# A selective scan on one core: dt's positive part and logarithm added up by TensorE, input scaling split in two places, SyncE's loads in written order

## The chip, the cores and the metric

The kernel runs on one core of a Trainium2 chip. The metric is device time in microseconds (us), from three runs of the unchanged kernel; lower is better. A core has TensorE (PE, matrix products into PSUM), VectorE (DVE), ScalarE (ACT), GpSimd (POOL) and SyncE (SP, which here only issues DMAs).

## The reference, cut to what matters

Four layers work on an image of shape (3, 256, 48, 48); the first three are an attention block and two 3x3 convolutions. The change touches only the fourth, a Mamba-style scan over the 2304 pixels of each image, with 512 inner channels and 16 states per channel:

```python
u  = silu(conv4(x_in))
dt = softplus(dt_raw @ dt_proj_w.T + dt_proj_b)
dA = exp(dt[:, :, None] * A)
h  = h * dA + dt[:, :, None] * B[:, None, :] * u[:, :, None]     # one step per pixel
y  = einsum('bdn,bn->bd', h, C) + u * D
out = (y * silu(z)) @ out_proj_w.T
```

The softplus is computed as log(1 + exp(x)) = max(x, 0) + log(1 + exp(-|x|)).

## The kernel before, in words

**Chunks and places.** The scan layer is cut into 18 chunks of 384 pixels (3 images x 6). A chunk runs 8 steps, one for each pair (m, h) of a block m of 128 channels and a half h of the states. A step does 8 scans on VectorE (`scan`, L1817), each of 385 columns. The text counts 16 places j in a chunk, four scans each: `j = 4*m + 2*h + part//4`. "Scan 13.0" is the first scan of place 13.

**The loop around a scan.** ScalarE makes the decay factors that a scan reads (`decay`, L1809: exp of dt times A) into one of three PSUM slots. A slot is free again when the scan that reads it has ended, so a decay can be at most three scans ahead. GpSimd and VectorE fill the scan tiles with dt*u*B before the scans (`fill`: L1779 and L1783 on GpSimd, L1765 on VectorE), and GpSimd multiplies the scanned states by C (`times_c`, L1834). TensorE adds the states up (L1851), and VectorE gates the sum (L1858).

**The next chunk's preparation** is spread over the scans of the current one. The list `plan` names for every stage its place j, its position in the place and how many chunks ahead it works. The positions are BEGIN, MID, DONE and LATE, after the place's scans 0, 1, 2 and 3, and PE_, after LATE (in odd places: at the step's end, after the filling and `times_c`). The stages that matter here, for the chunk one ahead:

- `project_dt(k, m0)` multiplies into the two PSUM banks `ps_g` for the channel blocks m0 and m0+1 (m0 is 0 or 2).
- `softplus(k, m0)` is on ScalarE: Abs of the two banks into `k.dt` (L1327), Exp (L1328) and Ln (L1329) of both at once.
- `take_dt(k, m0)` is on VectorE, for each of the two banks: max(x, 0) + logarithm back into the bank (L1343), then the bank times `k.u` into `k.dtu` (L1344), and three filler matmuls (`keep_busy`, L1336).
- `keep_dt(k, m0)` copies the banks to `k.dt` on ScalarE (L1349) and stores `k.dt` and three quarters of `k.dtu` in DRAM through SyncE's queue (`dtd`, L1353; `dtud`, L1355).
- `spread` (L1714) reads `dtd` and `dtud` back with rows repeated, eight DMAs on SyncE's queue for each m; `spread_second` (L1722) reads four more.

For the chunk two ahead, `group_scale` (L1213) applies a scale and shift to the input tile `xg`, one ScalarE operation for each of the two channel halves; `less_mean` (L1222) and `centre` (L1235, L1237) subtract the mean, using the same two banks `ps_g`.

**Fillers.** `keep_busy` issues 128x128 matmuls on the identity whose result nobody reads; the dictionary `busy` gives their places in the scan loop.

**Order.** `keep_order` binds each instruction of the scan layer on TensorE, VectorE, ScalarE and GpSimd to the one written before it, so these engines run in written order. SyncE is not in its list before the change. Waits between engines and on DMAs are set by the tile framework from what each instruction reads and writes; an instruction that overwrites a tile waits until a DMA that was issued earlier in the program has finished reading it. The first chunk is prepared before the layer starts (`early_preparation`, with the old `softplus` and `take_dt`), so the stages of `plan` that work one chunk ahead run 17 times.

Of the kernel before, what the change touches and what calls it, by code (L numbers as in the profile page):

```python
# [11 lines left out]
AF = mybir.ActivationFunctionType  # L12
ALU = mybir.AluOpType
# [3 lines left out]
P = 128  # L17
# [3 lines left out]
CT = 2  # L21
# [63 lines left out]
def net(  # L85
# [21 lines left out]
    nc = tc.nc  # L107
# [18 lines left out]
    ident = const.tile([P, P], F32, name="ident")  # L126
# [105 lines left out]
    listed = nc.cur_bb.bb.instructions  # L232
# [148 lines left out]
    with ExitStack() as l0:  # L381
# [36 lines left out]
        with ExitStack() as p1:  # L418
# [15 lines left out]
            for b in ORDER:  # L434
# [23 lines left out]
                for c in range(NCH):  # L458
                    for m, dst in ((0, y1), (1, cur[b])):
                        pm = ps.tile([P, 512], F32, tag="s", name="ps_y")  # L460
                        for ct in range(CT):
                            nc.tensor.matmul(  # L462
                                pm[:, :CH], ws[:, ct, m * P : (m + 1) * P], chunk(xb[:, ct, :], c),
                                start=ct == 0, stop=ct == CT - 1,
                            )
                        if c == 0 and m == 0:
# [3 lines left out]
                            bias=bb[:, m : m + 1], scale=b1sc[:, m : m + 1],  # L470
# [64 lines left out]
        with ExitStack() as p2:  # L535
# [9 lines left out]
            for i in range(NB):  # L545
# [400 lines left out]
                for mt in range(0, NT, 2):  # L946
                    pv = pair()
                    for j in range(2):
                        nc.tensor.matmul(
                            pv[:, j, :384], cur[2][:, (mt + j) * P : (mt + j + 1) * P], wn[2],  # L950
                            start=True, stop=True,
# [5 lines left out]
                mark = listed[-1]  # L957
# [3 lines left out]
                if exact:  # L961
                    k1 = keys(1)
                    attend_exact(2, k2)
                    k0 = keys(0)
                    attend_exact(1, k1)
                    attend_exact(0, k0)
                    at_once(mlp_weights(i, 2))
                    at_once(mlp_weights(i, 1))
                else:
                    attention({2: k2})  # L970
                    keep_order(tc, listed, mark)
# [76 lines left out]
        mark = listed[-1]  # L1048
# [45 lines left out]
        for _ in mixing:  # L1094
            pass
        keep_order(tc, listed, mark)
        for steps in small_steps:
            at_once(steps)
# [11 lines left out]
    def room(k, name):  # L1110
        return rooms[name][k.at % len(rooms[name])]
# [94 lines left out]
    bank = [t[:, :CH] for t in whole]  # L1206

    def group_scale(k):  # L1210
        sc, sh = norm3[k.b]
        for ct in range(CT):
            nc.scalar.activation(  # L1213
                k.xg[:, ct, :], k.xg[:, ct, :], AF.Identity,
                bias=sh[:, ct : ct + 1], scale=sc[:, ct : ct + 1],
            )
# [80 lines left out]
    def take_dbc(k):  # L1297

        dbc = k.dbc = room(k, "dbc")
        nc.scalar.activation(  # L1300
            dbc, bank[0][:96], AF.Identity, bias=ident[:96, DTR : DTR + 1]
        )
        bcd = dram.tile([2, DS, CH], F32, name="bcd")
        k.bc = []
        for j in range(2):
            nc.sync.dma_start(bcd[j], dbc[32 * (j + 1) : 32 * (j + 1) + DS, :])
            t = room(k, f"bc{j}")
            for i in range(4):
                src = bcd[j].rearrange("(g i) n -> i g n", i=4)[i : i + 1]
                nc.sync.dma_start(t[32 * i : 32 * i + 32], src.broadcast_to([32, 4, CH]))  # L1310
            k.bc.append(t)
        k.dt = room(k, "dt")
        k.dtu = room(k, "dtu")

    def project_dt(k, m0):
        for j in range(2):
            m = m0 + j
            nc.tensor.matmul(
                bank[j], w3v["dtsb"][:, m * P : (m + 1) * P], k.dbc[: DTR + 1, :],
                start=True, stop=True,  # L1320
            )

    def softplus(k, m0):

        both = k.dt[:, m0 : m0 + 2, :]
        for j in range(2):
            nc.scalar.activation(k.dt[:, m0 + j, :], bank[j], AF.Abs)  # L1327
        nc.scalar.activation(both, both, AF.Exp, scale=-1.0)  # L1328
        nc.scalar.activation(both, both, AF.Ln, bias=1.0)  # L1329
# [3 lines left out]
    def keep_busy(src, times):  # L1333

        for i in range(times if spread_tiles else 0):
            nc.tensor.matmul(  # L1336
                spread_tiles[-1][:, i % 2, CH:], ident, src, start=True, stop=True
            )

    def take_dt(k, m0):  # L1340
        for j in range(2):
            m, pdt = m0 + j, bank[j]
            nc.vector.scalar_tensor_tensor(pdt, pdt, 0.0, k.dt[:, m, :], ALU.max, ALU.add)  # L1343
            nc.vector.tensor_tensor(k.dtu[:, m, :], pdt, k.u[:, m, :], ALU.mult)  # L1344
            keep_busy(k.dtu[:, m, :P], 3)

    def keep_dt(k, m0):
        for j in range(2):
            nc.scalar.copy(k.dt[:, m0 + j, :], bank[j])  # L1349
        if m0 == 0:  # L1350
            k.dtd, k.dtud = {}, {}
        d = k.dtd[m0] = dram.tile([P, 2, CH], F32, name=f"dtd{m0}")
        nc.sync.dma_start(d, k.dt[:, m0 : m0 + 2, :])  # L1353
        d = k.dtud[m0] = dram.tile([3 * P // 4, 2, CH], F32, name=f"dtud{m0}")
        nc.sync.dma_start(d, k.dtu[P // 4 :, m0 : m0 + 2, :])  # L1355
# [27 lines left out]
    def store(k, mo):  # L1383
        nc.scalar.copy(k.ot[:, mo, :], k.y_out[mo])
        nc.sync.dma_start(
            out[k.b, mo * P : (mo + 1) * P, k.c * CH : (k.c + 1) * CH], k.ot[:, mo, :]
        )
# [2 lines left out]

    BEGIN, MID, DONE, LATE, PE_ = range(5)
    plan = [
        (12, MID, 2, group_scale),
        (12, PE_, 2, less_mean),
        (13, DONE, 2, centre),
        (13, PE_, 2, lambda k: keep_busy(ident, 5)),
        (13, PE_, 2, square_mean),
# [19 lines left out]
        (7, LATE, 1, lambda k: silu(k.u)),  # L1417
        (8, BEGIN, 1, project_u),
        (8, LATE, 1, take_dbc),
        (8, PE_, 1, lambda k: project_dt(k, 0)),  # L1420
        (9, LATE, 1, lambda k: softplus(k, 0)),
        (10, DONE, 1, lambda k: take_dt(k, 0)),
        (10, LATE, 1, lambda k: keep_dt(k, 0)),
        (10, PE_, 1, lambda k: project_dt(k, 2)),
        (11, LATE, 1, lambda k: softplus(k, 2)),
        (12, MID, 1, lambda k: take_dt(k, 2)),
        (12, DONE, 1, lambda k: keep_dt(k, 2)),
    ]

    after = [  # L1430
# [27 lines left out]
    def early_preparation():  # L1458
# [7 lines left out]
        while 2 not in norm3:  # L1466
            yield
        group_scale(k)
        yield
        less_mean(k)  # L1470
# [33 lines left out]
        for stage in (group_scale, less_mean, centre, square_mean, inverse_root, normalise):  # L1504
            stage(k)
            yield
# [7 lines left out]
        project_u(k)  # L1514
        yield
        take_dbc(k)
        yield
        for m in (0, 2):
            project_dt(k, m)
            yield  # L1520
            softplus(k, m)
            yield
            take_dt(k, m)
            yield
            keep_dt(k, m)
            yield
# [162 lines left out]
    with ExitStack() as l3:  # L1689
# [35 lines left out]
        def spread_pe(k, m):  # L1725

            t = psr.tile([P, 2, 512], F32, name="ps_r")
            for q in range(2):
# [10 lines left out]
        steps = [(at, m, h) for at in range(len(todo)) for m in range(DI) for h in range(2)]  # L1739
        tiles = {}  # L1740
        state = {}
        busy = {(2, 0, 3): 4, (2, 1, 1): 3, (2, 1, 2): 3, (2, 1, 3): 3, (2, 1, 5): 3,
                (3, 0, 0): 3, (3, 0, 1): 3, (3, 0, 2): 2}

        parts_of_step = [(g, q) for a in range(2) for g in range(2) for q in (2 * a, 2 * a + 1)]
        slots = [psd.tile([P, 512], F32, name=f"ps_da{i}") for i in range(3)]
# [113 lines left out]
        mark = listed[-1]  # L1860
        last = len(todo) - 1
        k = chunks[0]
# [7 lines left out]
        for s, (at, m, h) in enumerate(steps):  # L1870
            if m == 0 and h == 1 and at + 2 <= last:
                fetch(at + 2)
            for part in range(8):
                j = 4 * m + 2 * h + part // 4
# [38 lines left out]
        k = chunks[last]  # L1913
# [5 lines left out]
        for mo in range(2):  # L1919
            project_y(k, mo, DI - 1, DI)  # L1920
            store(k, mo)
        keep_order(tc, listed, mark)
    late_pools.close()


def keep_order(tc, listed, mark):

    engines = (
        mybir.EngineType.PE, mybir.EngineType.DVE, mybir.EngineType.Activation,
        mybir.EngineType.Pool,  # L1930
    )
    before = {}
    start = next(i for i in reversed(range(len(listed))) if listed[i] is mark)
    for ins in reversed(listed[: start + 1]):
        if ins.engine == mybir.EngineType.Activation:
            before[ins.engine] = ins.name
            break
    for ins in listed[start + 1 :]:
        e = ins.engine
        if e not in engines:  # L1940
            continue
        if e in before:
            tc.add_manual_dep(
                ins, before[e],
                mybir.DependencyInfo(mybir.DependencyClass.NoSync, mybir.DependencyReason.DATA),
                reason="order",
            )
        before[e] = ins.name


def net_kernel(tc, *args):

    with tc.tile_pool(name="flag", bufs=1) as pool:
        flag = pool.tile([1, 1], I32, name="flag")
        net(tc, *args, flag, False)
        bad = tc.nc.values_load(flag[:1, :1])
        with tc.If(bad > 0):
            net(tc, *args, None, True)
# [77 lines left out]
```

## Time and profile before

| what | value |
|---|---|
| median of 3 runs | 3374.56 us (3373.80 to 3378.72) |
| the profiled execution's own time | 3369.03 us |
| its span, first to last instruction | 3367.3 us |
| scans of the last layer, first to last start | 2013.8 to 3343.6 us |
| busy in 2300 to 2500 us: VectorE, GpSimd, PE, ScalarE | 198.5, 190.9, 186.4, 168.1 us |
| granted TensorE clock, whole span | 0.982 |

The scan layer takes about 1330 us, 74 us for each of the 18 chunks. Busy times of engines overlap and don't add up. A busy PE is not a PE at its peak, since matmuls are pipelined.

### The profile page before, as it was taken

How to read it: one execution, taken by the hardware profiler on the slowest of the kernel's cores; microseconds unless marked ns; L12 is line 12 of the kernel's file. 1: busy time of each engine (PE TensorE's matmuls, PEld its weight loads, DVE VectorE, ACT ScalarE, POOL GpSimd, SP SyncE). 2: the span in 40 equal slices, each digit the busy share in tenths (PEclk: the TensorE clock that was granted, in tenths of full speed). 3: DMA queues.
4: the chain of work that ended last, by engine and by line, in shares of the span. 5: the costliest groups of instructions: out<-in, count | busy, mean ns of one | idle time of the engine just before them, and what ended most of it. 6: DMA issues, size and time to landing. Idle time of an engine off the chain costs nothing.

```text
span 3367.3 us, 54979 instructions
## 1 busy us (share of the span) xinstructions
PE 3151.7 (94%) x21314; PEld 1586.5 (47%) x21314; DVE 2899.6 (86%) x3302; ACT 2375.1 (71%) x3596; POOL 1335.3 (40%) x457
## 2 busy tenths in 40 slices
PE   7999999999999999979999988999999999999985
PEld 4334343452333434547777764444444444444442
DVE  4799989959988997379976459999999999999997
ACT  3688888838888886332233548888888888888874
POOL 0000000000000000220000009999999999999997
PEclk9999999999999999989999999999999999999998
DMA  4000000010000002566611044555545555555552
GB/s 174 23 8 10 8 8 6 8 46 4 8 7 8 10 8 71 193 210 214 218 38 38 19 120 107 125 127 129 143 123 141 133 129 123 130 130 134 135 131 56
DMA packets 182165, 290.84 MB, mean 86 GB/s; under 512 B 34738, under 2 KB 148466, under 8 KB 179971
## 3 DMA queue, kind: packets, MB, share of 16 engines
q1 hardware_dynamic: 168658, 267.15, 29.6%
q10 hardware_dynamic: 13232, 20.06, 1.8%
q8 instruction: 169, 2.77, 0.4%
q14 instruction: 106, 0.86, 0.1%
HBM read 236.24 MB, written 50.64 MB: 85 GB/s over the span
## 4 chain that ended last, share of the span: by engine, by line
PE 52%; DVE 32%; ACT 7%; DMA 4%; issue 4%; SPq 1%; POOL 0%; ACTq 0%; DVEq 0%; POOLq 0%
DVE hs L1817 21%; PE ps_s L638 16%; PE acc L651 14%; PE ps_c L1546 8%; DVE hs L1765 3%; DVE u L296 2%; PE ps_y L462 2%; PE ps_m L665 2%; ACT ps_da L1809 2%; PE ps_s L1031 2%; PE ps_m L711 1%; PE acc L529 1%; PE ps_s L518 1%; DVE ps_g L1343 1%; DMA dtr<-dtd 1%
## 5 line engine op out<-in xcount | busy, mean ns | idle before, releaser
L642 ACT ACTIVATE pt<-ps_s 128x1024 f32<-128x1024 f32 x972 | 942.4, 1022 | 154.8 <-PE ps_s L638 142.1
L1817 DVE TENSOR_TENSOR_SCAN hs<-ps_da,hs 128x385 f32<-128x385 f32 x1152 | 1002.6, 936 | 5.1 <-ACT ps_da L1809 2.4
L857 DVE TENSOR_TENSOR part<-part,pt 128x2048 f32<-128x2048 f32 x396 | 906.6, 2289 | 41.2 <-ACT pt L642 18.5
L1809 ACT ACTIVATE ps_da<-dtr,u 128x384 f32<-128x384 f32 x1152 | 656.3, 582 | 191.3 <-DVE hs L1817 182.7
L164 POOL TENSOR_TENSOR rstd<-ve,mhalf 128x2 f32<-128x2 f32 (+1 forms) x26 | 16.3, 629 | 1473.4 <-DVE ve L162 1473.4
L638 PE MATMUL ps_s<-q,kt 32*128 32x512 f32 (+1 forms) x4320 | 576.4, 592 | 0.1
L651 PE MATMUL acc<-pt,vt 128*32 128x512 f32 (+1 forms) x4320 | 520.9, 561 | 0.2
L1546 PE MATMUL ps_c<-vt,u 128*128 128x288 f32 x1728 | 429.4, 409 | 21.0 <-DVE u L263 21.0
L1834 POOL TENSOR_TENSOR hc<-hs,x 128x3072 f32<-128x3072 f32 x72 | 405.2, 5628 | 30.8 <-DVE hs L1817 26.0
L1834 POOL TENSOR_TENSOR hc<-hs,bc 128x3072 f32<-128x3072 f32 x71 | 400.1, 5635 | 24.7 <-DVE hs L1817 23.0
L1546 PEld LDWEIGHTS ps_c<-vt,u 128*128 128x128 f32 x1728 | 328.9, 191 | 116.6 <-issue 19.8
L638 PEld LDWEIGHTS ps_s<-q,kt 32*128 32x128 f32 x4320 | 195.3, 183 | 199.1 <-issue 120.2
L651 PEld LDWEIGHTS acc<-pt,vt 128*32 128x32 f32 x4320 | 94.4, 108 | 353.4 <-issue 326.7
L1851 PE MATMUL ps_y<-hc,u 128*32 128x384 f32 x2304 | 228.1, 516 | 2.8 <-POOL hc L1834 2.8
L1273 PE MATMUL ps_g<-u 128*128 128x384 f32 x576 | 196.2, 494 | 23.4 <-ACT u L1269 23.4
L1783 POOL TENSOR_TENSOR hs<-dtur,x 128x1536 f32<-128x1536 f32 x72 | 209.0, 2903 | 8.3 <-DMA dtur<-dtud 8.3
L1783 POOL TENSOR_TENSOR hs<-dtur,bc 128x1536 f32<-128x1536 f32 x72 | 209.3, 2907 | 1.3 <-DMA dtuq<-dtud 0.9
L1273 PEld LDWEIGHTS ps_g<-u 128*128 128x128 f32 x576 | 108.8, 191 | 107.7 <-ACT u L1269 34.6
L1336 PE MATMUL ps_r<-hs,ident 128*128 128x128 f32 x864 | 130.9, 292 | 27.3 <-DVE hs L1817 27.2
L1336 PEld LDWEIGHTS ps_r<-hs,ident 128*128 128x128 f32 x864 | 107.6, 192 | 80.8 <-DVE hs L1817 63.0
L1851 PEld LDWEIGHTS ps_y<-hc,u 128*32 128x32 f32 x2304 | 62.0, 112 | 144.5 <-issue 130.4
L1562 ACT COPY cb<-ps_c 128x288 f32<-128x288 f32 x48 | 19.1, 398 | 154.5 <-PE ps_c L1546 140.4
(266 smaller groups left out, 4051.0 us busy)
## 6 DMA issues: line engine op xcount, KB each, us to landing
wconv<-in_we SPq DMA_DIRECT2D x144, 384.0 KB, 4.2
dtr<-dtd SPq DMA_DIRECT2D x288, 192.0 KB, 3.9
dtur<-dtud SPq DMA_DIRECT2D x288, 96.0 KB, 4.3
wconv<-xd SPq DMA_DIRECT2D x36, 384.0 KB, 3.7
x<-bcd SPq DMA_DIRECT2D x72, 192.0 KB, 5.1
dtd<-x SPq DMA_DIRECT2D x36, 384.0 KB, 2.9
dtuq<-dtud SPq DMA_DIRECT2D x288, 48.0 KB, 2.0
bc<-bcd SPq DMA_DIRECT2D x72, 192.0 KB, 4.8
```

What stands on the lines that cost most here:

```text
L638: nc.tensor.matmul(s[:, j, cols], kt[r, mt * P : (mt + 1) * P], q[r, :n], start=True, stop=True,)
L642: nc.scalar.activation(p[:, h0 : h0 + 2, :], s, AF.Exp)
L651: nc.tensor.matmul(acc[h * HD : (h + 1) * HD, :n], vt[:, mt, g * P + h * HD : g * P + (h + 1) * HD], p[:, h, cols], start=mt == 0, stop=mt ...
L857: ): nc.vector.tensor_tensor(part, first, p, ALU.add)
L1273: nc.tensor.matmul(bank[m % 2], w3v["taps"][:, m, tap, :], w3v["xi"][:, m % 3, tap : tap + CH], start=tap == 0, stop=tap == DCONV - 1,)
L1336: nc.tensor.matmul(spread_tiles[-1][:, i % 2, CH:], ident, src, start=True, stop=True)
L1546: nc.tensor.matmul(pc[:, :HN], u[:, i, dy, ct, m * P : (m + 1) * P], vt[:, i, ct, dy * TW : dy * TW + HN], start=ct == 0 and dy == 0, stop ...
L1783: nc.gpsimd.tensor_tensor(states(s)[:, :, 2:4, 1:], chunks[at].rows[m][1].unsqueeze(1).broadcast_to([P, 2, 2, CH]), b_rows(s, 0, 2), ALU.mult,
L1809: nc.scalar.activation(slots[n % 3][:, 1 : CH + 1], chunks[at].rows[m][0][:, q, :], AF.Exp, scale=amat[:, col : col + 1],)
L1817: nc.vector.tensor_tensor_scan(b, slots[(8 * s + part) % 3][:, : CH + 1], b, 0.0, ALU.mult, ALU.add)
L1834: nc.gpsimd.tensor_tensor(hc, tiles[s][:, :, :, 1:], cb.broadcast_to([P, 2, 4, CH]), ALU.mult)
L1851: nc.tensor.matmul(k.y_ps[32 * q : 32 * q + 32, :CH], fold, hc[:, g, q, :], start=False, stop=h == 1 and g == 1,)
```

## The change

The second addition of the softplus leaves VectorE. ScalarE writes the positive part (Relu) into `k.dtu` and the absolute value into `k.dt`; Exp and Ln follow as before, in place. TensorE adds both into the two banks with the identity as the weights (`sum_dt`: part 0 the positive part, part 1 the logarithm). VectorE only multiplies the sum by `k.u` (`take_sum`). The stages get new places: `keep_dt(k, 0)` goes from place 10 to 11, `project_dt(k, 2)` from 10 to 11, and in the second half `keep_dt(k, 2)`, at place 12 LATE, stands before `take_sum(k, 2)`, at place 13 BEGIN. In the first half `take_sum` stands before `keep_dt`.

`group_scale` runs at places 6 and 7, one half each, instead of both halves at place 12. `less_mean` goes from 12 PE_ to 13 MID. The three fillers behind each multiplication go, and `busy` holds 16 fillers for each chunk instead of 24. In `take_dbc` both stores stand before the eight loads. SyncE's DMAs of the scan layer are now bound to written order too.

```diff
-    def group_scale(k):
+    def group_scale(k, *cts):
         sc, sh = norm3[k.b]
-        for ct in range(CT):
+        for ct in cts or range(CT):
...
         for j in range(2):
             nc.sync.dma_start(bcd[j], dbc[32 * (j + 1) : 32 * (j + 1) + DS, :])
+        for j in range(2):
             t = room(k, f"bc{j}")
...
+    def relu_of(k, m0):
+        for j in range(2):
+            nc.scalar.activation(k.dtu[:, m0 + j, :], bank[j], AF.Relu)
+
+    def abs_of(k, m0):
+        for j in range(2):
+            nc.scalar.activation(k.dt[:, m0 + j, :], bank[j], AF.Abs)
+
+    def relu_abs(k, m0):
+        for j in range(2):
+            nc.scalar.activation(k.dtu[:, m0 + j, :], bank[j], AF.Relu)
+            nc.scalar.activation(k.dt[:, m0 + j, :], bank[j], AF.Abs)
+
+    def exp_of(k, m0):
+        both = k.dt[:, m0 : m0 + 2, :]
+        nc.scalar.activation(both, both, AF.Exp, scale=-1.0)
+
+    def log_of(k, m0):
+        both = k.dt[:, m0 : m0 + 2, :]
+        nc.scalar.activation(both, both, AF.Ln, bias=1.0)
+
+    def sum_dt(k, m0, part):
+        src = (k.dtu, k.dt)[part]
+        for j in range(2):
+            nc.tensor.matmul(
+                bank[j], ident, src[:, m0 + j, :], start=part == 0, stop=part == 1
+            )
+
+    def take_sum(k, m0):
+        for j in range(2):
+            m = m0 + j
+            nc.vector.tensor_tensor(k.dtu[:, m, :], bank[j], k.u[:, m, :], ALU.mult)
+
...
             nc.vector.tensor_tensor(k.dtu[:, m, :], pdt, k.u[:, m, :], ALU.mult)
-            keep_busy(k.dtu[:, m, :P], 3)
...
-        (12, MID, 2, group_scale),
-        (12, PE_, 2, less_mean),
+        (6, BEGIN, 2, lambda k: group_scale(k, 0)),
+        (7, BEGIN, 2, lambda k: group_scale(k, 1)),
+        (13, MID, 2, less_mean),
...
         (8, PE_, 1, lambda k: project_dt(k, 0)),
-        (9, LATE, 1, lambda k: softplus(k, 0)),
-        (10, DONE, 1, lambda k: take_dt(k, 0)),
-        (10, LATE, 1, lambda k: keep_dt(k, 0)),
-        (10, PE_, 1, lambda k: project_dt(k, 2)),
-        (11, LATE, 1, lambda k: softplus(k, 2)),
-        (12, MID, 1, lambda k: take_dt(k, 2)),
-        (12, DONE, 1, lambda k: keep_dt(k, 2)),
+        (9, DONE, 1, lambda k: relu_of(k, 0)),
+        (9, LATE, 1, lambda k: abs_of(k, 0)),
+        (10, BEGIN, 1, lambda k: sum_dt(k, 0, 0)),
+        (10, DONE, 1, lambda k: exp_of(k, 0)),
+        (11, BEGIN, 1, lambda k: log_of(k, 0)),
+        (11, MID, 1, lambda k: sum_dt(k, 0, 1)),
+        (11, LATE, 1, lambda k: take_sum(k, 0)),
+        (11, LATE, 1, lambda k: keep_dt(k, 0)),
+        (11, PE_, 1, lambda k: project_dt(k, 2)),
+        (11, PE_, 1, lambda k: relu_abs(k, 2)),
+        (11, PE_, 1, lambda k: exp_of(k, 2)),
+        (12, BEGIN, 1, lambda k: sum_dt(k, 2, 0)),
+        (12, BEGIN, 1, lambda k: log_of(k, 2)),
+        (12, MID, 1, lambda k: sum_dt(k, 2, 1)),
+        (12, LATE, 1, lambda k: keep_dt(k, 2)),
+        (13, BEGIN, 1, lambda k: take_sum(k, 2)),
...
-        busy = {(2, 0, 3): 4, (2, 1, 1): 3, (2, 1, 2): 3, (2, 1, 3): 3, (2, 1, 5): 3,
-                (3, 0, 0): 3, (3, 0, 1): 3, (3, 0, 2): 2}
+        busy = {(2, 0, 3): 4, (2, 1, 1): 2, (2, 1, 2): 2, (2, 1, 3): 3, (2, 1, 4): 3,
+                (3, 0, 3): 2}
...
-        keep_order(tc, listed, mark)
+        keep_order(tc, listed, mark, True)
...
-def keep_order(tc, listed, mark):
+def keep_order(tc, listed, mark, loads=False):
...
-    )
+    ) + ((mybir.EngineType.SP,) if loads else ())
```

## The prediction

> **What bounds the kernel now.** I read first the windows (busy time of each engine in a stretch of the scan layer), then VectorE's groups by shape within that layer, then what VectorE waited for there. Columns of a window: length, busy us (x instructions) of PE, PEld, DVE, ACT, POOL, then granted clock, DMA share, GB/s.
>
> ```profile
> 2300.00:2500.00 200.00, 186.40 (x920) 96.08 (x918) 198.47 (x239) 168.09 (x323) 190.87 (x55) 1.00 0.55 133
> ...
> 3280.00:3300.00 20.00, 12.92 (x63) 4.74 (x63) 20.00 (x24) 16.31 (x27) 20.00 (x6) 0.68 0.44 100
> ```
> ```profile
> L1817 DVE TENSOR_TENSOR_SCAN hs<-ps_da,hs 128x385 f32<-128x385 f32 x1152 | 1002.6, 936 | 5.1 <-ACT ps_da L1809 2.4 <-POOL hs L1783 0.8 <-issue 0.4
> ...
> L1343 DVE SCALAR_TENSOR_TENSOR ps_g<-ps_g,x 128x384 f32<-128x384 f32 x68 | 37.7, 555 | 3.0 <-ACT x L1329 3.0
> ```
> VectorE is busy 198.5 of 200 us. Over the layer (2014 to 3344 us) its waits add up to some 14 us of 1330. So what VectorE no longer does shortens the span nearly one for one, and so does every wait put into its queue lengthen it. GpSimd stands close behind (190.9): the gain has a floor there, 1330 - 1267 (its busy time in the layer) = about 60 us away. The last lines of the first view show the layer's end, where the preparation has run out: PE 12.9 of 20 us busy and the clock at 0.68.
>
> The path that the change touches besides is SyncE's queue. Its timeline in one chunk, where the second half of dt leaves (columns: start, us, queue and line, out<-in, count):
>
> ```profile
> 2448.45 0.33 SPq L1353 DMA_DIRECT2D dtd<-x  x1
> 2448.88 2.44 SPq L1714 DMA_DIRECT2D dtr<-dtd  x4
> 2451.42 1.79 SPq L1714 DMA_DIRECT2D dtur<-dtud  x4
> 2453.31 0.37 SPq L1355 DMA_DIRECT2D dtud<-x  x1
> ```
> The `dtud` store goes out behind eight loads. The DMA table of the layer gives 4.4 to 4.5 us from its issue to its landing (all 36: 3.2 to 5.9); `dtd` takes 2.9, `dtr` 3.9. In the old order nothing on VectorE waits for it.
>
> **What the skill says here.** "Perfetto Trace Analysis", Identifying the Most-Contended Engine: occupancy is a fair measure for VectorE; the trace agrees, its waits are 1% of the layer. "DMA: Bandwidth & Descriptors", Anatomy of one DMA: about 2 us are fixed, mostly the confirmation of the last byte, and the wait for a semaphore is made by the issuing sequencer. The trace's smallest store (`bcd`, 24 KB, 1.6 us) fits. "ScalarE: Activation LUTs", What ACT_TABLE_LOAD costs: an operation with immediate operands 186 ns + 0.833 per column, 93 ns of it overlapped, so an estimated 413 ns for 384 columns; the Abs pairs of L1327 take 0.85 us, 0.425 each. "TensorE: Matmul & The Clock Gate", Part 1: an idle window of about 3.4 us halves the clock. The 0.68 above, where PE has gaps, agrees.
>
> **The change part by part, for one chunk (17 are prepared so).**
>
> *VectorE's additions go:* 4 x L1343 at 0.555 = 2.22 us, and their waits, 3.0/17 = 0.18. **-2.4 us.**
>
> *ScalarE gets 4 Relus* at 0.425 (Abs as nearest row) = 1.7 us. ScalarE is busy 168 of 200 us and waits for VectorE 183 us in the layer, so most of it lies in idle time. At places 9 to 11, however, I walked the order: scans start every 6.90/8 = 0.86 us and last 0.93, a decay takes 0.58, the copy of first states 0.19. The Relus, Abs, Exp and Ln now stand one or two between decays, and every decay still comes in time for its scan, but the Ln of the first half ends about 3.3 us after scan 11.0 starts. The two sums follow on PE (0.9 us for the first, 0.64 more for the second, as L1372 and L1374 show), so the second is there 0.5 us after VectorE could use it (scan 11.3 ends at 3.5, the gate at 4.0, the first multiplication at 4.5). **+0.5 us** (0 to 1).
>
> *PE:* 8 sums of 0.64 to 0.9 = 5 to 7 us come, 20 fillers of 0.3 us (L1336: 12 records, two for each, in 1.78 us) = 6 us go. Nearly even, beside VectorE's work: 0. The bound both ways is in the clock below.
>
> *`group_scale`:* two operations of 0.69 us move from place 12 to 6 and 7, where ScalarE waits about 0.27 us at each decay for VectorE; 0, hidden there. Its input was fetched at place 2 and lands within 4.2 us, some 15 us before. Without that cover it would be 0.69 twice.
>
> *SyncE in order, and the two stores before the loads:* no DMA is added. SyncE spends 0.44 us on an issue, about 70 a chunk, so some 31 of 74 us, and waited 200 us each at L1353, L1385 and L1714 for ScalarE: it has room. 0, with 0 to +0.5 as bounds.
>
> *The store before the multiplication.* In the second half `keep_dt` issues the `dtud` store from `k.dtu`, and `take_sum` then overwrites the same rows. As built, the first multiplication waits for that store to complete. I walk the queues, with zero at the start of scan 11.0. Last scan of place 11 ends at 3.5, gate and two multiplications to 5.05, filling (2.6) to 7.65, scans 12.0 to 13.0 end at **12.05**: there VectorE is ready for `take_sum(k, 2)`. The store: ScalarE copies the first half after VectorE's multiplications, to 5.65; `dtd` (first half) goes out at 5.7 and lands at 8.6 (2.9). The four `dtr` loads wait for it: 8.7 to 10.7 with the issue times above; the `dtur` loads wait for `dtud`'s first half (about 10.2), so they go out from 10.8 to 12.6. Meanwhile ScalarE does Relu and Abs twice, Exp (0.84), decay, Ln, three decays and the two copies, to 12.85. So `dtd` (second) goes at 12.9, `dtud` at 13.3 to 13.7, and lands 4.5 us later, at **18**. VectorE waits 18.0 - 12.05 = **+5.9 us** (4.5 where it lands as fast as the fastest, 7.2 with the slowest). Behind the multiplication in VectorE's queue are scan 13.1 and all the rest; ScalarE's decays wait for those scans, PE's `less_mean` for the bank, GpSimd for the states. There is no other work to cover it, since VectorE is the bound. The half-microsecond above shifts both ends alike.
>
> *PE after it:* in that wait PE has two fillers and then nothing for about 5.8 us. If an idle window falls in it, the clock halves, the four `less_mean` products (2.6 us) become slower, `centre` on ScalarE waits for them and decay 14.2 behind it comes late; my walk leaves it 0.1 us of slack. **+0.7 us** taken (half of the chunks, 1.4 us), 0 to 2.5 as bounds.
>
> Sum: -2.4 + 0.5 + 5.9 + 0.7 = **+4.7 us a chunk**, x 17 = +80 us. On the profiled execution: 3369 + 80 = 3449. That run lies 5.5 us under the median of the three, and the difference is carried over: 3374.6 + 80 = **3454 us**.
>
> **Rivals.** *A, the wait is hidden, and the additions' gain stays.* The store would have to land before 12.05 on that scale, so leave by 7.5; it stands behind the eight loads and the second half's copies, which end at 12.85. For it: my order of SyncE's waits could be too strict, or the wait could not bind. It decides for faster as soon as the wait is under 2.4 - 0.5 - 0.7 = 1.2 us. At no wait and no clock loss: -1.9 x 17 = -32, 3342 us. *B, a short wait eats the gain:* about 1.9 us, with no clock loss; 3375. The walk would have to be wrong by 4 us. *C, SyncE's written order brings the row loads late too:* 72 spreads, each 0.5 us, +36 on the forecast; 3490. Against it: the orders of the loads differ little, and the first spread of a chunk is loaded 10 us before its decay. It would show as decays that wait for `dtr`.
>
> **How the numbers follow.** Forecast 0.85, A 0.07, B 0.03, C 0.05. The lowest of the forecast's own bounds: -2.4 + 0 + 4.5 + 0 = 2.1 a chunk, +36, 3410; the highest -2.4 + 1 + 7.2 + 2.5 = 8.3, +141, 3515, which needs all at their worst. The range is 3405 to 3500; it takes in C and leaves out A, B and the worst corner. About 0.2% (7 us) is what a measurement of this kernel can tell from no change. Faster 0.07, same 0.03, slower 0.90.
>
> **What would show it.** Right: the line of `take_sum` has 17 waits of about 6 us for the `dtud` DMA and becomes the largest wait on VectorE; VectorE's busy time falls by 38 us although the span grows; SyncE's timeline shows `dtd` and `dtud` of the second half behind eight loads; the clock dips once in many chunks after place 13. The waits of `take_sum`'s first half, for PE, are under 1 us. Wrong: no VectorE wait for a DMA at that line (A), waits of 2 us (B), ScalarE's decays waiting for `dtr` (C), or new waits of the scans for decays at places 9 to 12, which would mean that ScalarE's bursts, taken as hidden, are not.

## The result, and the profile after

The changed kernel takes 3460.91 us (median of four runs, 3457.19 to 3463.45) beside 3374.18 us for the kernel before: a ratio of 1.0258 (95% interval 1.0245 to 1.0271), 2.6% slower, 86.7 us. The forecast was 3454 us.

The profiled execution of the changed kernel took 3463.45 us. Its scans start at 2021.5 us, 7.7 us later than before. 7.0 of these are there when the convolutions' first product starts (1518.2 against 1511.2 us), ahead of any changed code; that is the executions' own difference. From the first scan's start to the last one's it is 1416.7 us against 1329.8, **86.9 us more**, which is the whole difference of the medians.

The windows again (length, busy us of PE, PEld, DVE, ACT, POOL, clock, DMA share, GB/s):

```profile
2300.00:2500.00 200.00, 174.42 (x796) 88.89 (x795) 176.37 (x212) 155.30 (x310) 175.38 (x52) 0.94 0.52 126
...
3400.00:3420.00 20.00, 14.03 (x72) 6.35 (x71) 20.00 (x24) 12.13 (x23) 20.00 (x6) 0.83 0.42 105
```
VectorE has fallen from 198.5 to 176.4 us of 200, in the middle of the layer, and every other engine with it. The clock is 0.94 there now; it was 1.00. In the layer's last stretch, where no preparation runs, VectorE is busy throughout as before. So VectorE waits, once for every chunk that is prepared. For what, the list of its waits shows (us in total, times, longest):

```profile
DVE dtu L1355 <- DMA dtud<-dtu: 51.4, 9, 6.0
DVE x L1355 <- DMA dtud<-x: 50.2, 8, 7.0
DVE hs L1860 <- ACT ps_da L1852: 30.7, 19, 2.3
```
The first two are one wait: the multiplication `take_sum(k, 2)` on the `dtud` store of the same rows, 17 times, 101.6 us, **5.98 us each**. (`k.dtu` lies in one of two rooms, and the trace names them `dtu` and `x`.) The third is new too: scans that wait for their decay, 30.7 us; before it was 2.4.

VectorE's groups in the layer, with the additions gone and the scans as long as before:

```profile
L1860 DVE TENSOR_TENSOR_SCAN hs<-ps_da,hs 128x385 f32<-128x385 f32 x1152 | 1002.3, 934 | 32.6 <-ACT ps_da L1852 30.7 <-POOL hs L1826 0.6
...
L1355 DVE TENSOR_TENSOR dtu<-ps_g,u 128x384 f32<-128x384 f32 x36 | 18.3, 549 | 51.4 <-DMA dtud<-dtu 51.4
```
And one chunk of the timeline, all engines, cut to the chain that matters (start, us, engine, line, out<-in, then idle time before it and what ended it):

```profile
2471.42 0.34 SPq L1386 DMA_DIRECT2D dtd<-x  x1
2471.86 0.38 SPq L1388 DMA_DIRECT2D dtud<-x  x1
2473.34 4.34 DVE L1860 TENSOR_TENSOR_SCAN hs<-ps_da,hs 128x385 f32<-128x385 f32 x5
...
2474.36 1.75 SPq L1757 DMA_DIRECT2D dtr<-dtd  x4
...
2476.22 1.77 SPq L1757 DMA_DIRECT2D dtur<-dtud  x4
...
2477.38 0.85 ACT L1382 COPY x<-ps_g 128x384 f32<-128x384 f32 x2
...
2478.25 0.34 SPq L1386 DMA_DIRECT2D dtd<-x  x1
2478.64 0.43 SPq L1388 DMA_DIRECT2D dtud<-x  x1
...
2483.23 1.02 DVE L1355 TENSOR_TENSOR x<-ps_g,x 128x384 f32<-128x384 f32 x2 [5.55 <-DMA dtud<-x]
...
2483.84 4.96 PE L1222 MATMUL ps_g<-wconv,u 128*128 128x384 f32 x8 [5.81 <-DVE x L1355]
...
2488.08 0.48 ACT L1235 COPY wconv<-ps_g 128x384 f32<-128x384 f32 x1 [1.44 <-PE ps_g L1222]
```
Read from the top: the first half's stores go out, VectorE does its five scans (12.0 to 13.0) and is done at 2477.7. At that time SyncE has nearly issued the eight loads (the last is out at 2477.99). The second half's `dtd` then waits for ScalarE's copies (L1382), which end at 2478.23, and leaves at 2478.25; the `dtud` store follows at 2478.64 and lands 4.5 us later. Only then the multiplication starts. It is the same in most chunks: in 14 of the 17 the loads are out 0.2 to 1.8 us before the second `dtd`, which leaves within 0.03 us of the copies' end; in the other three the loads end last or level with the copies. PE's four products of `less_mean` (eight records) behind the wait take 4.96 us, and ScalarE waits for them. In the kernel before they take 2.85 us in all 16 chunks that have them; in the changed kernel 4.3 to 5.5 us, again in all 16.

One thing the times don't show. By the code, the second half's store takes `k.dtu` while it holds the positive part, max(x, 0), and the product overwrites it afterwards. `spread` and `spread_second` read these rows back as dt*u for the blocks 2 and 3. So for these rows the changed kernel leaves out the logarithm and the multiplication by u: it isn't the reference's scan any more. The same holds for every kernel below that keeps `keep_dt(k, 2)`, or its store, ahead of `take_sum(k, 2)`.

### The profile page after: what moved, and what is told of

Same layout as the page of the kernel before. It is cut to its first block, busy times and chain, and to the rows that moved or that the text cites. A ratio compares the mean times of both kernels' runs of the same rounds, so it can differ in the third digit from the quotient of the medians.

```text
span 3461.6 us, 54162 instructions
## 1 busy us (share of the span) xinstructions
PE 3177.4 (92%) x20890; PEld 1574.4 (45%) x20890; DVE 2862.5 (83%) x3234; ACT 2392.9 (69%) x3664; POOL 1334.3 (39%) x457
## 4 chain that ended last, share of the span: by engine, by line
PE 56%; DVE 27%; ACT 8%; DMA 5%; issue 4%; SPq 0%; POOL 0%; ACTq 0%; DVEq 0%; POOLq 0%
DVE hs L1860 18%; PE ps_s L638 16%; PE acc L651 14%; PE ps_c L1589 8%; DVE hs L1808 3%; PE ps_g L1222 2%; ACT ps_da L1852 2%; PE ps_s L1031 2%; PE ps_y L462 2%; DVE u L296 2%; PE ps_m L665 1%; PE ps_m L711 1%; PE acc L529 1%; PE ps_s L518 1%; DMA dtud<-dtu 1%
## 5 line engine op out<-in xcount | busy, mean ns | idle before, releaser
L1860 DVE TENSOR_TENSOR_SCAN hs<-ps_da,hs 128x385 f32<-128x385 f32 x1152 | 1002.3, 934 | 32.6 <-ACT ps_da L1852 30.7
L1222 PE MATMUL ps_g<-wconv,u 128*128 128x384 f32 x144 | 85.6, 766 | 91.0 <-DVE x L1355 47.4
```

Source lines behind the costliest of these rows:

```text
L1222: nc.tensor.matmul(bank[to], w3v["less"][:, int(to != ct), :], k.xg[:, ct, :], start=ct == 0, stop=ct == CT - 1,)
L1860: nc.vector.tensor_tensor_scan(b, slots[(8 * s + part) % 3][:, : CH + 1], b, 0.0, ALU.mult, ALU.add)
```

## The experiments

All times are medians; ratios are to runs of the kernel before on the same chip, with their 95% intervals. The edits are to the changed kernel unless the text says otherwise.

**The multiplication ahead of the store.**

```diff
-        (12, LATE, 1, lambda k: keep_dt(k, 2)),
         (13, BEGIN, 1, lambda k: take_sum(k, 2)),
+        (13, BEGIN, 1, lambda k: keep_dt(k, 2)),
```


> The changed kernel, but in the second half the multiplication (take_sum) stands before the copies and the two stores (keep_dt), both at place 13 BEGIN; the store then carries the product. Theory (the 17 waits of 6 us on the dtud store are the loss, and the slower less_mean behind them follows from the idle gap): VectorE's 101.6 us of waits for dtud go, and about 28 of the 31 us in which scans wait for decays; 3461 - 102 - 28 = about 3331 us, faster than before by 1.3%. Rival (the new ScalarE and PE work at places 9 to 13 is too much by itself and the wait only hides it): the scans' waits for decays stay or grow, and the time stays above 3374 us. Rival 2 (only the stall goes, the clock still dips because of the missing fillers): about 3359 us.

Measured: 3333.12 us, ratio 0.9883 (0.9867 to 0.9900). Two lines exchanged are worth 128 us against the changed kernel, and the result is 1.2% faster than the kernel before. Here the store carries the product, so the rows that are read back are dt*u again. VectorE's window and its waits in this kernel:

```profile
2300.00:2500.00 200.00, 190.27 (x904) 94.62 (x902) 197.87 (x235) 175.17 (x343) 196.66 (x57) 0.99 0.53 129
```
```profile
DVE hs L1860 <- ACT ps_da L1852: 5.9, 15, 1.9
...
DVE x L1355 <- PE ps_g L1348: 1.9, 2, 0.9
DVE dtu L1355 <- PE ps_g L1348: 1.9, 2, 0.9
```
The multiplication waits for no DMA any more, and the scans' waits have fallen from 30.7 to 5.9 us with it. The theory holds, both rivals fall. GpSimd is now busy 196.7 of 200 us, level with VectorE.

**The store ahead of the loads and the copies.** The store still stands ahead of the multiplication, with the positive part; only its place in SyncE's queue changes. It no longer follows the second half's `dtd`.

```diff
         nc.sync.dma_start(d, k.dt[:, m0 : m0 + 2, :])
+        if m0 not in k.dtud:
+            store_dtu(k, m0)
+
+    def store_dtu(k, m0):
...
         (11, PE_, 1, lambda k: relu_abs(k, 2)),
+        (11, PE_, 1, lambda k: store_dtu(k, 2)),
```


> The changed kernel with one DMA moved: the dtud store of the second half is issued right behind the Relus at the end of place 11, ahead of the eight row loads, and take_sum still stands behind it (the store carries the positive part, as in the changed kernel). Theory (the wait is long because the store leaves behind eight loads and the second half's copies, so it lands 6 us late): the store now lands at about 11 us on the prediction's scale, before VectorE arrives at 12.05, the waits fall from 6 us to under 0.5 us each, and the time is about that of the kernel with the multiplication first, 3331 us. Rival (an overwrite behind a store costs by itself, wherever the store stands; or the early store in SyncE's order holds back the loads behind it): waits of 2 us or more stay at take_sum, or decays wait for dtr; 3370 us or more.

Measured: 3335.81 us, ratio 0.9897 (0.9880 to 0.9913). The multiplication's line, in its two rooms:

```profile
L1355 DVE TENSOR_TENSOR dtu<-ps_g,u 128x384 f32<-128x384 f32 x36 | 18.4, 550 | 3.2 <-ACT x L1382 3.1
L1355 DVE TENSOR_TENSOR x<-ps_g,x 128x384 f32<-128x384 f32 x32 | 16.5, 551 | 3.3 <-ACT x L1382 2.9 <-PE ps_g L1348 0.2
```
Of the waits, 6.5 us are left in all, and the profile puts nearly all of them down to ScalarE's copies; none is for the store. So here the overwrite behind a store cost nothing by itself, once the store had landed before VectorE arrived. The 6 us were the place of the store in the queue. This experiment moves it ahead of two things at once, the eight loads and the `dtd` store with its wait for the copies. The timeline above tells them apart as far as is known: in 14 of 17 chunks the copies ended after the loads were out, so moving the loads alone would have gained little there. No run moves the loads alone.

**Fillers in the gap, 16 and then 22.** These kernels keep the 6 us wait and ask for the clock.

```diff
         (12, LATE, 1, lambda k: keep_dt(k, 2)),
+        (12, PE_, 1, lambda k: keep_busy(ident, 16)),     # the second kernel: 22
```


> The changed kernel with 16 more fillers on PE (0.3 us each, 4.7 us) at place 12 PE_, in the gap in which VectorE waits for the dtud store. Theory (PE's idle gap halves the clock, less_mean becomes slow and the decays behind centre come late): the clock stays near 1.00 through the gap, the scans' waits for decays fall from 31 us to under 10, the dtud waits stay at 102 us; 3461 - 25 = about 3436 us. Rival (those decays are late because less_mean starts late, whatever the clock): the waits of 31 us stay and the time is unchanged or a little longer.

Measured: 3445.22 us, ratio 1.0224 (1.0207 to 1.0241). The waits for decays fell to 13.8 us, not under 10: the direction of the theory, short of its size. The fillers were shorter than expected: the 32 records of 16 fillers take 3.74 us in a row, not 4.7. They left gaps of 1.0 to 3.9 us before `less_mean`. Its products still take 4.3 to 5.5 us in 9 of the 16 chunks, behind gaps of 2.1 to 3.9 us, and 2.85 us in the other 7, behind gaps of 1.0 to 2.05 us.

> The kernel with fillers in the gap, but 22 fillers (6.5 us, the whole gap) instead of 16 (4.7 us). Theory (the idle window that is left after 16 fillers still halves the clock in some chunks, 13.8 us of scans' waits): those waits fall to under 5 us, 3435 us. Rival (less_mean's late start alone makes the rest): they stay at 10 us or more, and the fillers that last longer than the gap hold less_mean back: 3445 us or more.

Measured: 3434.34 us, ratio 1.0185 (1.0168 to 1.0202). The theory holds; the 22 fillers take 5.08 us. The VectorE waits:

```profile
DVE dtu L1355 <- DMA dtud<-dtu: 55.8, 9, 7.8
DVE x L1355 <- DMA dtud<-x: 48.2, 8, 6.6
...
DVE hs L1861 <- ACT ps_da L1853: 4.2, 4, 2.1
```
The store waits are as before (104 us), the decay waits are gone but for 4.2 us (the products are slow in one chunk of 16, 4.54 us), and the granted clock of the middle windows is 0.98 to 0.99 again, without any change in what PE computes for the result. The 26.6 us between the changed kernel and this one are the price of the clock, to within some 7 us by the intervals of the two ratios. What it did to the products behind the gap, the group of `less_mean` in the changed kernel shows:

```profile
L1222 PE MATMUL ps_g<-wconv,u 128*128 128x384 f32 x128 | 80.0, 800 | 90.5 <-DVE x L1355 47.4 <-DVE dtu L1355 43.1
```
and the same group in the kernel before:

```profile
L1222 PE MATMUL ps_g<-wconv,u 128*128 128x384 f32 x128 | 45.6, 499 | 5.0 <-ACT x L1349 5.0
```
0.80 instead of 0.50 us for each record. The Trainium skill's "TensorE: Matmul & The Clock Gate", Part 1, says that an idle window of about 3.4 us halves the clock. In the changed kernel the products behind PE's gap, 4.6 to 7.3 us long, were slow every time, 5.8 us in the chunk shown. But in the kernel with 16 fillers they were slow behind all eight gaps of 2.1 to 3.3 us too: here less than the page's 3.4 us of idle time was enough.

**The other parts alone, on the kernel before.** First SyncE's order with the two stores ahead of the loads, then `group_scale` at places 6 and 7.

```diff
-        keep_order(tc, listed, mark)
+        keep_order(tc, listed, mark, True)
```


> The kernel before with SyncE's DMAs bound to written order and both bcd stores before the loads, nothing else. Theory (SyncE has room, its order costs nothing): 3374 us, within 0.2%. Rival C (rows come late too): decays wait for dtr and the time rises by some 0.5 us for each of 72 spreads, 3410 us. Rival (the order helps, loads leave earlier): VectorE's waits of 14 us can't shrink by more than that, so 3360 us at best.

Measured: 3370.53 us, ratio 0.9996 (0.9987 to 1.0005): no difference, as the theory said.

```diff
-        (12, MID, 2, group_scale),
+        (6, BEGIN, 2, lambda k: group_scale(k, 0)),
+        (7, BEGIN, 2, lambda k: group_scale(k, 1)),
```


> The kernel before with only group_scale moved from place 12 to places 6 and 7. Theory (its two operations are hidden in ScalarE's idle time in both places): 3372 us as before, within 0.2%, VectorE's waits for decays stay under 5 us in the layer. Rival (at places 6 and 7, ahead of the Silu with its two table loads, they make decays late): 0.69 us or more of scans' waits in each of 16 chunks, 3383 us or more.

Measured: 3372.11 us, ratio 0.9998 (0.9989 to 1.0007): no difference either, with 2.7 us of scans' waits for decays.

**dt's sum without the other parts.** These start from the kernel with the multiplication first. Both edits together, with the `bcd` stores between the loads again, are the first kernel; the next two take back one of them each.

```diff
-        (6, BEGIN, 2, lambda k: group_scale(k, 0)),
-        (7, BEGIN, 2, lambda k: group_scale(k, 1)),
+        (12, MID, 2, group_scale),
...
-        keep_order(tc, listed, mark, True)
+        keep_order(tc, listed, mark)
```


> The kernel with the multiplication first, without the two other parts: group_scale at place 12 as before, SyncE's loads and the bcd stores as before. Theory (the gain is VectorE's four additions, 2.4 us in each of 17 chunks, and the other parts only don't hurt): 3333 us plus what group_scale's 1.4 us cost among the Relus, Abs, Exp and Ln at place 12, up to 17 x 1.4 = 24; 3333 to 3357 us. Rival (the written order of SyncE's loads is what makes the rearranged stages work): above 3357 us, with waits of decays for dtr or of fills for rows.

Measured: 3346.03 us, ratio 0.9919 (0.9902 to 0.9935), 12.9 us more than with all parts and inside the theory's range; the rival's 3357 us is not reached.

> The kernel with the multiplication first, with group_scale back at place 12 (both halves, MID), SyncE in written order as there. Theory (the 13 us by which dt's sum alone, 3346, stays behind the full set, 3333, come from group_scale's 1.4 us among the Relus, Exp and Ln): about 3345 us, with some 5 us more of scans' waits for decays and of the multiplications' waits for PE. Rival (they come from SyncE's order): 3333 us.

Only `group_scale` back: 3343.62 us, 0.9915 (0.9898 to 0.9931). The multiplications' waits for PE are 7.6 us (3.8 with the early scaling), the decays' 8.3 (5.9).

> The kernel with the multiplication first, with group_scale at places 6 and 7, but SyncE not bound to written order and the bcd stores between the loads as before. Theory (SyncE has room): 3333 us, within 0.2%. Rival (the 13 us come from SyncE's order): about 3345 us.

Only SyncE's order back: 3335.89 us, 0.9892 (0.9876 to 0.9909), against 0.9883 with the order: no difference that these intervals tell. So some 10 of the 13 us are `group_scale`'s, which costs nothing in the old schedule and does in the new one. That it is because the new ScalarE work stands at place 12 is argued: the waits named here grew by 6 us.

**Fillers, all and none.** Both are edits to the kernel with the multiplication first.

> The kernel with the multiplication first, with all of the old fillers put back (24 for each chunk in the scan loop, three behind each multiplication). Theory (half of the fillers can go because the sums keep PE as busy): 3333 us, within 0.2%, the clock 0.99 to 1.00 in both. Rival (the fillers are still needed: clock dips cost something at the 15 waits for decays): up to 6 us faster. Rival 2 (fillers plus sums hold PE's queue back, so the sums and the multiplications come late): 3345 us or more.

```diff
             nc.vector.tensor_tensor(k.dtu[:, m, :], bank[j], k.u[:, m, :], ALU.mult)
+            keep_busy(k.dtu[:, m, :P], 3)
...
-        busy = {(2, 0, 3): 4, (2, 1, 1): 2, (2, 1, 2): 2, (2, 1, 3): 3, (2, 1, 4): 3,
-                (3, 0, 3): 2}
+        busy = {(2, 0, 3): 4, (2, 1, 1): 3, (2, 1, 2): 3, (2, 1, 3): 3, (2, 1, 5): 3,
+                (3, 0, 0): 3, (3, 0, 1): 3, (3, 0, 2): 2}
```
Measured: 3375.91 us, ratio 1.0009 (1.0000 to 1.0018): the whole gain is gone, 43 us. The theory (same time) falls, and the time is that of the second rival. VectorE's largest waits there:

```profile
DVE hs L1809 <- PE ps_r L1371: 20.8, 17, 1.2
DVE hs L1861 <- ACT ps_da L1853: 16.6, 18, 1.2
```
The filling (L1809) waits for a filler (L1371), 17 times: fillers write into the tile `ps_r` that the filling reads, and stand in PE's queue among the sums. These 20.8 us, 10.7 more of waits for decays and 2.6 more of the multiplications' waits for PE make 34 of the 43 us; for the rest no line was found. The second rival's own path, late multiplications, is the smallest part. The clock was 0.99 to 1.00 with the fillers.

> The kernel with the multiplication first, without the 16 fillers of each chunk in the scan loop (the five ahead of square_mean stay). Theory (all old fillers cost 42 us because they stand in PE's queue ahead of the sums and hold the PSUM tile that VectorE's filling reads; with half of them nothing on VectorE waits for a filler any more, so fewer gain nothing, and PE's gaps now halve the clock in some chunks): 3333 to 3350 us, granted clock lower than 0.98. Rival (each filler costs, 20 fewer gained 42 us): some 30 us faster, 3300 us.

```diff
-        busy = {(2, 0, 3): 4, (2, 1, 1): 2, (2, 1, 2): 2, (2, 1, 3): 3, (2, 1, 4): 3,
-                (3, 0, 3): 2}
+        busy = {}
```
Measured: 3345.15 us, ratio 0.9923 (0.9906 to 0.9940), slower than with 16 by 12 us, at a clock of 0.93 to 0.97 in the middle windows. The multiplications' waits for PE grew from 3.8 to 12.5 us. That is inside the theory's range; the rival (faster still) falls. Of the three counts, 16 in the scan loop is better than the old set and than none.

## Why the prediction was right, point by point

**VectorE's additions, -2.4 us a chunk.** Right. With the wait removed, the layer's scans take 1293.2 us from first to last start, 36.6 less than before. 17 x 2.4 is 41; the waits that are new (3.5 us more for decays, 3.8 for PE) would leave 33.5, so it holds to some 3 us.

**The first half's sum late by 0.5 us.** It wasn't. In the changed kernel the multiplications don't wait for PE to speak of, since the Ln ended some 0.8 us earlier than I walked it (2468.5, or 2.5 us after scan 11.0 began). With the multiplication first it is 3.8 us in all, 0.2 a chunk.

**The wait on the store, +5.9 us.** Measured 5.98 on average (5.4 to 7.0), and each point of the walk was close. In the chunk shown, whose wait is 5.55, on the same scale (zero at the start of scan 11.0, 2466.0), forecast and measured: VectorE ready at 12.05 and 11.7; first stores out at 5.7 and 5.4; first load 8.7 and 8.4; last load issued by 12.6 and 12.0; copies done at 12.85 and 12.2; the `dtud` store out at 13.3 to 13.7 and 12.6; landing after 4.5 and 4.5. All but the landing time were some 0.3 to 1 us early, on both sides, so the difference held; that the errors had the same sign is in part luck. The kernel with the early store shows that the walk had the right cause, the store's place in the queue. It also had the right order of the two things ahead: the copies end last, shortly after the loads.

**The clock behind the gap, +0.7 us.** The mechanism was right, the size was off. I took half of the chunks at 1.4 us. Measured: 28.3 us more waits for decays, 1.7 a chunk, and 26.6 us by the filler experiment. The half was the wrong part: the products behind the gap are slow in all 16 chunks, by 1.4 to 2.6 us each.

**PE's exchange of 20 fillers for eight sums, 0.** With the multiplication first, PE is busy 190.3 of 200 us, beside 186.4 before: nearly even, as forecast (a filler takes 0.23 us in a row, not the 0.3 that was taken). But the term is not small because PE's work is beside VectorE's anyway: with the sums and all the fillers the kernel loses 43 us. Taking the fillers out is a condition of the gain.

**`group_scale` and SyncE's order, 0.** Right for both on the kernel before. In the rearranged schedule `group_scale`'s new place is worth about 10 us, which the prediction had not looked for.

The sum was +4.7 a chunk and +80 us; the terms as measured, -2.4 + 0 + 6.0 + 1.7, give 5.3 a chunk and 90 us, and the layer showed 86.9. Rival A (3342 us) did not happen, but its number is near that of the kernels in which the store no longer makes VectorE wait: 3333 and 3336 us.

## What to carry to other kernels

An overwrite in place waits for a DMA that was issued earlier from the same bytes (here 17 times of 17), so ask of each store where it stands in its queue, what the DMAs ahead of it wait for, and when the engine behind it will want those bytes; on the bounding engine a two-line exchange was worth 128 us. Ask too what the bytes hold when the store leaves: here the order that made VectorE wait also stored the wrong value. When work moves between engines, walk the queues of all of them with measured durations from one zero: here both ends of a wait were off by up to a microsecond the same way, and the wait was still right. Fillers that keep a clock up occupy the queue and the tile that they write: here none (3345 us) and the old set (3376 us) were both slower than 16 a chunk (3333 us).

## What the runs showed of the hardware that I had not expected

PE's gap before `less_mean`, 4.6 to 7.3 us long, cost 1.6 us behind it in the average of all chunks. 16 fillers of 3.7 us in all were not enough to prevent it: 13.8 us of waits were left, since gaps of 2.1 us and more remained in 9 chunks of 16. With 22 fillers, 5.1 us, 4.2 us were left.
